# A graph layer on one core: q's node rows picked by one-hot matmuls, receivers of a group in one DMA, edge features in four pieces

## The chip, the cores and the metric

The kernel runs on one core of one Trainium2 chip. The metric is device time in microseconds (us). Before the change it is 2856.44 us, the median of three runs (2854.62 to 2858.7).

## The reference

One layer of message passing on a graph of 6,250 nodes (rows of `x`, 128 features, 8 heads of 16) and 206,250 edges, sorted by receiver. Each edge has a sender, a receiver, a weight and two sets of 32 features.

```
w_ij  = silu(edge_attr_32 @ rad_W1 + rad_b1) @ rad_W2 + rad_b2
      + silu(edge_attr_32_n2 @ sph_W1 + sph_b1) @ sph_W2 + sph_b2
q_i   = (x @ Wq)[receivers]; k_j = (x @ Wk)[senders]; v_j = (x @ Wv)[senders]
alpha = sum over a head's 16 features of q_i * w_ij * k_j, / 4, * edge_weight
out   = segment_sum(alpha * v_j, receivers) / 16
result = layernorm(x + out)          # no scale, no shift
```

All of it is float32. The inputs come sorted by receiver, so the receivers of neighbouring edges lie in a narrow band of nodes.

## The kernel before

**Units.** A tile has 128 edges, a quad four tiles (512 edges), a group four quads (2,048 edges). There are 101 groups (g = 0 to 100) and 403 quads. Within a group the quads go in the order 0, 2, 1, 3, which are slots 0 to 3 of the loop. Quads 0 and 2 (slots 0 and 1) form one pair for the hidden layers, quads 1 and 3 the other.

**Before the loop.** `x` is turned and multiplied with Wk and Wv; the rows of k and v go to a table in DRAM, `kv_tab`. `tables` (L252) works out small tables: for each quad the first node of a window of 32 nodes (`qb`), for each group the first node of a window of 128 nodes (`gb`). The receiver numbers relative to the quad's window (`rel`) are also turned and stored in DRAM (`rel_lin`).

**The loop.** An edge's q is not gathered. For each group the 4 x 32 rows of x of its quads' windows are loaded (`load_q`, L153: four DMAs of 32 rows, each with its start read into a register of SP, L117), turned by one transpose on TensorE (`turn_q`, L336, copied to SBUF by ScalarE at L338) and multiplied with Wq (`make_q`, L344, L346). `take_q` (L388) then multiplies q's 32 rows with a one-hot matrix of the receivers (`hotT`, L350, made by VectorE from `relb`, the receivers spread over 32 partitions per quad by `load_rel`, L145, in four DMAs).

For a quad, TensorE runs the hidden layers of both feature sets (`hidden`, L367: contraction over 32 rows, so the two quads of a pair use four separate strips of rows), ScalarE takes the silu (L372), TensorE multiplies by the second weights (`weigh`, L379) and ScalarE adds the bias (L381). VectorE multiplies by q (L393), TensorE turns the product back to edges in rows (`turn_back`, L399), VectorE multiplies by k (L404), sums per head (L406), multiplies by the weight (L407) and multiplies v by the result (`messages`, L415). TensorE adds the messages by receiver with one-hots (`sum_quads`, L425), a group's sums are placed in its window of 128 nodes and joined with those of the group before (`sum_group`, L446, L448, ScalarE's copy `tot` at L450), and `statistics` (L463 and on) adds the window's rows of x (`xw`, loaded by `load_xw`, L452) and normalizes. The rows go out to DRAM for four groups at a time (L479), in slot 2 of the groups with g % 4 = 1.

**What sets the order.** Each engine's order is the order of the code (a manual schedule); semaphores are derived from it. SP issues all plain DMAs in that order too, one after another: a DMA that has to wait for its buffer holds back those behind it. In slot 0 of group g SP gets `load_q(g+1)`, `load_xw(g-1)` and `load_rel(g+1)`, in slot 1 `load_feats(g+2)`. Most tiles of a group have two buffers, so `feats` of group g+2 goes where that of group g was. GpSimd issues only the gathers of k and v (L113): four DMAs per quad, 14 quads ahead of their use, into a ring of 16 buffers; the four gathers of a new quad wait until `messages` (L415) has read the buffer. The four `ph` buffers in PSUM are shared in turn by hidden layers, `weigh`, `sum_group`, `turn_q` and `make_q`.

Where TensorE's work is placed in a slot:

```
w = weigh(q)
if before is not None:
    pu = turn_back(before)
pq = take_q(q)
if slot % 2 == 0:
    ...
        hidden(pairs[u])
if slot == 1 and 2 <= g:
    sum_group(g - 2)
if slot == 1 and g + 1 < NG:
    turn_q(g + 1)
if slot == 3:
    make_q(g + 1)
```

`sum_quads(g - 1, ...)` follows in every slot from the second group on, and then VectorE's work.

Of the kernel before, what the change touches and what calls it, by code (L numbers as in the profile page):

```python
# [22 lines left out]
P = 128  # L23
N = 6250
# [27 lines left out]
def gnn_kernel(ctx, tc, x, src, dst, weight, edges, rad_W1, rad_b1, rad_W2, rad_b2,  # L52
# [35 lines left out]
    ones = const.tile([P, P], F32, name="ones")  # L88
    eps = const.tile([P, 1], F32, name="eps")
    rel = const.tile([P, NT], F32, name="rel")  # L90
    qb_i = const.tile([1, NG * NQ], I32, name="qb_i")
    gb_i = const.tile([1, NG], I32, name="gb_i")
    rowq = const.tile([P, NG], F32, name="rowq")
    rowp = const.tile([P, NG], F32, name="rowp")
    gb = const.tile([P, NG], F32, name="gb")
# [28 lines left out]
    for q in order:  # L124
        if q % NQ < 2:
            pairs.append([q])
        else:
            pairs[-1].append(q)
    feats_of, relb_of, act_of, kv_of, hot_of, hotT_of, xq_of, q_of, msg_of = ({} for _ in range(9))
    po_of, part_of, to_of, tot_of, xw_of, y0_of, u_of = ({} for _ in range(7))  # L130

    def gathers(q):
        kv = quad_of("kv", RING, 2 * D)
# [1 line left out]
            gather(kv[:, t, :], kv_tab, src_i[:, q * QT + t:q * QT + t + 1])  # L135
        kv_of[q] = kv

    def load_feats(g):
        feats_of[g] = gp.tile([P, EG // 2], F32, name="feats")
        nc.sync.dma_start(feats_of[g], edges[g])  # L140

    def quads_in(g):
        return min(NQ, QUADS - g * NQ)

    def load_rel(g):  # L145

        relb_of[g] = gp.tile([P, EQ], BF16, name="relb")
        for j in range(NQ):
            t = g * GT + j * QT
            nc.sync.dma_start(relb_of[g][j * W:(j + 1) * W, :],  # L150
                              rel_lin[t:t + QT, :].rearrange("t e -> (t e)").partition_broadcast(W))

    def load_q(g):  # L153

        xq_of[g] = gp.tile([P, D], F32, name="xq")
        for j in range(quads_in(g)):
            r = start_of(qb_i, g * NQ + j, N - W)
            nc.sync.dma_start(xq_of[g][j * W:(j + 1) * W, :], x[ds(r, W), :])

    manual = ctx.enter_context(ExitStack())  # L160
    manual.enter_context(tc.manual_schedule())
# [15 lines left out]
    with tc.tile_pool(name="nodes", bufs=1) as nodes, \  # L177
            tc.tile_pool(name="nodes_ps", bufs=2, space=PSUM) as nps:
        chunks = [(c, min(QT, NB - c)) for c in range(0, NB, QT)]
        quads_x = order[:XQ]  # L180
        xs_of, xT_of = {}, {}
        smalls = []
        for i, (w, b, bb) in enumerate(((rad_W2, rad_b1, rad_b2), (sph_W2, sph_b1, sph_b2))):
            smalls += [(w2[:, i, :], w), (b1[:, i:i + 1], b[:, None]), (b2[:, i:i + 1], bb[:, None])]
# [1 line left out]
            smalls.append((w1[i * R:(i + 1) * R, :], w))  # L186


        def load_x(k):
# [61 lines left out]

        def tables():  # L252
            nc.vector.tensor_scalar(gb, qb[:, :, 0], float(N - P), None, op0=OP.min)
            nc.vector.tensor_copy(qb_i, qb[:1].rearrange("p g j -> p (g j)"))
            nc.vector.tensor_copy(gb_i, gb[:1])
            load_q(0)
            for j in range(NQ):
                b = slice(j * W, (j + 1) * W)
                nc.vector.tensor_scalar(roww[b, :], row[b, :], float(j * W), None, op0=OP.subtract)
                nc.vector.tensor_tensor(rowq[b], qb[b, :, j], gb[b], op=OP.subtract)  # L260
            nc.vector.tensor_scalar(rowq, rowq, roww, None, op0=OP.add)
            nc.vector.tensor_copy(rowwp, roww)
            nc.vector.tensor_copy(colp, col)

# [31 lines left out]
        for _ in range(12):  # L296
            nc.tensor.transpose(warm[:, :P], ident, ident)
        for k in range(8):
            load_x(k)
# [5 lines left out]
        for i, (k, n) in enumerate(work):  # L305
            if i + 2 < len(work):
                turn(*work[i + 2])
            kvs = k_and_v(k, n)
            for o, w in smalls[i:i + 1]:
                nc.scalar.dma_start(o, w)  # L310
            if i >= len(chunks):
                kv_of[k[0]] = kvs
                continue
            store(k, kvs)
            if k + 8 < len(chunks):
                load_x(k + 8)
# [13 lines left out]


    with tc.tile_pool(name="ps", bufs=1, space=PSUM) as pp:
        def turn_q(g):
            n = quads_in(g) * W
            pt = pp.tile([P, EQ], F32, name="ph", bufs=4)
            nc.tensor.transpose(pt[:, :n], xq_of[g][:n, :], ident[:n, :n])  # L336
            xq_of[g] = gp.tile([P, P], F32, name="xqT")
            nc.scalar.activation(xq_of[g][:, :n], pt[:, :n], AF.Copy)  # L338

        def make_q(g):  # L340

            n = quads_in(g) * W
            pt = pp.tile([P, EQ], F32, name="ph", bufs=4)
            nc.tensor.matmul(pt[:n, :D], xq_of[g][:, :n], wq, start=True, stop=True)  # L344
# [14 lines left out]
        def hidden(pair):  # L359

            for q in pair:
                g, j = divmod(q, NQ)
                r0, c0 = 2 * R * (j // 2), EQ * (j % 2)
                for i in range(2):
                    ph = pp.tile([P, EQ], F32, name="ph", bufs=4)
                    r = slice(r0 + i * R, r0 + (i + 1) * R)
                    nc.tensor.matmul(ph, w1[r, :], feats_of[g][r, c0:c0 + EQ], start=True, stop=True)  # L367
                    act_of[q, i] = ph
            for q in pair:
                for i in range(2):  # L370
                    act = ep.tile([P, EQ], F32, name="act", bufs=8)
                    nc.scalar.activation(act, act_of[q, i], AF.Silu, bias=b1[:, i:i + 1])  # L372
                    act_of[q, i] = act
# [75 lines left out]
            tot_of[g] = gp.tile([P, D], F32, name="tot")  # L449
            nc.scalar.activation(tot_of[g], ph[:, :D], AF.Copy)  # L450

        def load_xw(g):  # L452
            r = start_of(gb_i, g, N - P)
            xw_of[g] = gp.tile([P, D], F32, name="xw")
            nc.sync.dma_start(xw_of[g], x[ds(r, P), :])

        def statistics(g):
            first = g // LB * LB if g < NG - 2 else g
            if g == first:
                y0_of[g] = (gp.tile([P, LB, D], F32, name="y0"), gp.tile([P, LB, 2], F32, name="mv"))  # L460
            y0, mv = y0_of[first]
            k = g - first + 1
            nc.vector.tensor_tensor(y0[:, k - 1, :], tot_of[g], xw_of[g], op=OP.add)  # L463
            st = gp.tile([P, 6], F32, name="st")
            nc.vector.bn_stats(st, y0[:, k - 1, :])
            nc.vector.bn_aggr(mv[:, k - 1, :], st)
            if k == LB or g >= NG - 3:
                sd = gp.tile([P, LB], F32, name="sd")
                nc.scalar.activation(sd[:, :k], mv[:, :k, 1], AF.Sqrt, bias=eps)
                rs = gp.tile([P, LB], F32, name="rs")  # L470
                nc.vector.reciprocal(rs[:, :k], sd[:, :k])
                shift = gp.tile([P, LB], F32, name="shift")
                nc.vector.scalar_tensor_tensor(shift[:, :k], mv[:, :k, 0], -1.0, rs[:, :k],
                                               op0=OP.mult, op1=OP.mult)
                for i in range(k):
                    nc.scalar.activation(y0[:, i, :], y0[:, i, :], AF.Identity,  # L476
                                         scale=rs[:, i:i + 1], bias=shift[:, i:i + 1])
                    r = start_of(gb_i, first + i, N - P)
                    nc.sync.dma_start(out[ds(r, P), :], y0[:, i, :])  # L479
# [16 lines left out]
        def verdict():  # L496
# [4 lines left out]
            nc.vector.tensor_reduce(found, pe[:1, :8], AX.X, OP.add)  # L501
            nc.vector.tensor_scalar(general, found, 0.0, None, op0=OP.is_gt)

        turn_q(0)
        make_q(0)
        one_hots_T(0)
# [5 lines left out]
        for g in range(NG):  # L512
            last = g == NG - 1
            for slot, j in enumerate((0, 2, 1, 3)):
# [32 lines left out]
                before = q  # L547
                if slot == 0:
                    if g + 1 < NG:
                        load_q(g + 1)  # L550
                    if 1 <= g:
                        load_xw(g - 1)
                        if g + 1 < NG:
                            load_rel(g + 1)
                if slot == 1:
                    if g + 2 < NG:
                        load_feats(g + 2)
                    if 1 <= g:
                        place(g - 1)
                    if last:  # L560
                        place(g)
                        load_xw(g)
# [179 lines left out]
```

## Time and profile before

| | |
|---|---|
| median of three runs | 2856.44 us |
| the profiled execution | 2843.93 us |
| its span, first to last instruction | 2841.9 us |
| mean granted TensorE clock | 0.847 |
| gathers of k and v, GpSimd, 1,580 | 1498.5 us busy, 948 ns each |
| `weigh`, TensorE, 1,612 instructions | 961.9 us busy, 726 ns each |
| hidden layers, TensorE, 1,612 | 626.3 us busy, 726 ns each |
| `take_q`, TensorE, 806 | 475.8 us busy, 671 ns each |
| silu, ScalarE, 806 | 500.4 us busy |
| VectorE, all | 1412.9 us busy |
| DMA | 310.42 MB, 109 GB/s on average |
| DMA issues of `feats` | 101, 512 KB each |
| DMA issues of `relb` | 404, 32 KB each |
| DMA issues of `xq` / `xw` | 403, 16 KB each / 101, 64 KB each |

How to read the profile's lines: a group of instructions has its line in the kernel, its engine, the operation, output and input tiles, the count after an x, then busy time in us, the mean of one in ns, and after the next bar the idle time of that engine just before them with what ended most of it. PE is TensorE, PEld its weight loads, DVE VectorE, ACT ScalarE, POOL GpSimd, SP SyncE; "q" behind an engine is its queue of DMA issues. A float32 matmul stands in the trace as two instructions, a transpose as one. Ends of matmuls are modelled. "issue" is idle time for which no releaser shows, "remote" one whose releaser is unknown. The row PEclk gives the granted TensorE clock in tenths for 40 slices of the span. A timeline lists start, duration, engine, line, operation and, in brackets, the idle time before it. A view of windows gives each engine's busy time in stretches between two times, the granted clock, the share in which the DMA engines are busy, and GB/s.

### The profile page before, as it was taken

Reading aid. Unit: us, or ns where it says so; the run is one execution under the profiler, and the core shown is the slowest. Engines: PE = TensorE matmul, PEld = TensorE weight load, DVE = VectorE, ACT = ScalarE, POOL = GpSimd, SP = SyncE. Lnnn points to the kernel's source line nnn. Section 1 sums busy time; section 2 is a strip of 40 time slices with the busy share of each in tenths; the row PEclk is TensorE's granted clock in tenths of the full one; section 3 lists DMA queues with packets and bytes.
Section 4 is the critical chain, followed back from the end, with each engine's and each line's share of the span. In section 5 each row is a group of like instructions: output and inputs, shape, how many; then the busy total and the mean of one; then the engine's idle time right before and its main releaser. Section 6 shows DMA issues by size and latency. Waiting matters only on the chain. (4 is left out here: it accounts for less than half of the span.)

```text
span 2841.9 us, 32012 instructions
## 1 busy us (share of the span) xinstructions
PE 2310.3 (81%) x9843; PEld 1023.9 (36%) x9843; DVE 1412.9 (50%) x2874; ACT 1000.3 (35%) x1826; POOL 1530.0 (54%) x1620
## 2 busy tenths in 40 slices
PE   5578878878887888888888888888888878788887
PEld 4333333333333333333333333333333333333333
DVE  3244554555554544545454454554544545455456
ACT  1233333333332433333333343333333333333334
POOL 4455555555555555555555555555555555555540
PEclk7788988888788887878888888888888888888889
DMA  5433333333333333333333333333334333333330
GB/s 175 133 111 97 118 105 114 113 102 111 118 105 111 102 118 102 110 111 104 110 107 112 116 98 110 119 102 120 108 99 119 103 106 116 107 112 113 108 99 26
DMA packets 166844, 310.42 MB, mean 109 GB/s; under 512 B 46530, under 2 KB 99212, under 8 KB 166668
## 3 DMA queue, kind: packets, MB, share of 16 engines
q0 software_dynamic: 76864, 209.29, 25.4%
q1 hardware_dynamic: 88316, 98.64, 10.5%
q8 instruction: 79, 1.29, 0.2%
q14 instruction: 97, 0.79, 0.1%
q10 hardware_dynamic: 1488, 0.40, 0.1%
HBM read 294.70 MB, written 13.46 MB: 108 GB/s over the span
## 5 line engine op out<-in xcount | busy, mean ns | idle before, releaser
L113 POOL DMA_INDIRECT kv<-kv_tab,src_i x1580 | 1498.5, 948 | 1217.7 <-DVE msg L415 748.5
L379 PE MATMUL ph<-act,w 128*128 128x512 f32 x1612 | 961.9, 726 | 95.8 <-ACT act L372 73.5
L404 DVE TENSOR_TENSOR m<-pu,kv 128x512 f32<-128x512 f32 x403 | 278.7, 691 | 1240.3 <-remote 434.1
L367 PE MATMUL ph<-feats,w 32*128 32x512 f32 x1612 | 626.3, 726 | 259.6 <-ACT w L381 198.4
L372 ACT ACTIVATE act<-ph,b 128x512 f32<-128x512 f32 x806 | 500.4, 688 | 317.6 <-PE ph L367 222.8
L381 ACT ACTIVATE w<-ph,bsum 128x512 f32<-128x512 f32 x403 | 276.9, 687 | 758.4 <-PE ph L379 286.7
L379 PEld LDWEIGHTS ph<-act,w 128*128 128x128 f32 x1612 | 325.1, 224 | 524.0 <-issue 367.4
L388 PE MATMUL pq<-hotT,q 32*128 32x512 f32 x806 | 475.8, 671 | 2.6 <-issue 2.6
L367 PEld LDWEIGHTS ph<-feats,w 32*128 32x128 f32 x1612 | 202.8, 206 | 454.9 <-ACT w L381 269.6
L399 PEld LDWEIGHTS pu<-ident,u 128*128 128x128 f32 x1612 | 215.1, 151 | 350.9 <-issue 200.6
L399 PE MATMUL pu<-ident,u 128*128 128x128 f32 x1612 | 259.5, 286 | 86.5 <-DVE u L393 83.7
L393 DVE TENSOR_TENSOR u<-pq,w 128x512 f32<-128x512 f32 x403 | 274.8, 682 | 55.1 <-PE ph L367 39.6
L406 DVE TENSOR_REDUCE side<-m 128x32 f32<-128x512 f32 x403 | 280.1, 695 | 13.7
L415 DVE TENSOR_TENSOR msg<-kv,side 128x512 f32<-128x512 f32 x403 | 273.0, 677 | 0.0
L425 PE MATMUL po<-msg,hot 128*32 128x128 f32 x3224 | 173.1, 312 | 2.9 <-ACT part L441 2.9
L450 ACT ACTIVATE tot<-ph 128x128 f32<-128x128 f32 x101 | 28.0, 277 | 399.3 <-remote 138.2
L388 PEld LDWEIGHTS pq<-hotT,q 32*128 32x128 f32 x806 | 123.2, 191 | 76.4 <-issue 76.4
L425 PEld LDWEIGHTS po<-msg,hot 128*32 128x32 f32 x3224 | 77.6, 117 | 154.2 <-issue 136.7
L407 DVE TENSOR_TENSOR side<-side,scale 128x32 f32<-128x32 f32 x403 | 80.4, 199 | 13.8
L346 ACT ACTIVATE q<-ph 128x128 f32<-128x128 f32 (+1 forms) x101 | 28.0, 277 | 144.8 <-issue 66.1
L350 DVE TENSOR_TENSOR hotT<-relb,side 128x512 f32<-128x512 bf16 x101 | 68.8, 681 | 0.0
L355 DVE TENSOR_TENSOR hot<-rel,side 128x512 f32<-128x512 f32 x101 | 68.8, 681 | 0.0
(83 smaller groups left out, 813.2 us busy)
## 6 DMA issues: line engine op xcount, KB each, us to landing
feats<-in_edges SPq DMA_DIRECT2D x101, 512.0 KB
kv<-kv_tab,src_i POOLq DMA_INDIRECT x1580
relb<-rel_lin SPq DMA_DIRECT2D x404, 32.0 KB
xw<-in_x SPq DMA_DIRECT2D x101, 64.0 KB
out<-y SPq DMA_DIRECT2D x101, 64.0 KB
xq<-in_x SPq DMA_DIRECT2D x403, 16.0 KB
kv_tab<-kv SPq DMA_DIRECT2D x12, 512.0 KB
act<-in_x SPq DMA_DIRECT2D x12, 256.0 KB
```

Of the source, the lines that this page charges most:

```text
L113: nc.gpsimd.indirect_dma_start(out=o, out_offset=None, in_=table, in_offset=bass.IndirectOffsetOnAxis(ap=index, axis=0))
L367: nc.tensor.matmul(ph, w1[r, :], feats_of[g][r, c0:c0 + EQ], start=True, stop=True)
L372: nc.scalar.activation(act, act_of[q, i], AF.Silu, bias=b1[:, i:i + 1])
L379: nc.tensor.matmul(pw, w2[:, i, :], act_of[q, i], start=(i == 0), stop=(i == 1))
L381: nc.scalar.activation(w, pw, AF.Identity, bias=bsum)
L388: nc.tensor.matmul(pq, q_of[g][b, :], hotT_of[g][b, :], start=True, stop=True)
L393: nc.vector.tensor_tensor(u_of[q], pq, w, op=OP.mult)
L399: nc.tensor.transpose(pu[:, t, :], u_of[q][:, t * P:(t + 1) * P], ident)
L404: nc.vector.tensor_tensor(m, pu, kv_of[q][:, :, :D], op=OP.mult)
L406: nc.vector.tensor_reduce(alpha, m.rearrange("p t (h e) -> p t h e", e=HD), AX.X, OP.add)
L415: nc.vector.tensor_tensor(msg_of[q].rearrange("p t (h e) -> p t h e", e=HD), kv_of[q][:, :, D:].rearrange("p t (h e) -> p t h e", e=HD), a ...
L425: nc.tensor.matmul(po_of[g][j * W:(j + 1) * W, :], hot_of[g][:, j * QT + t, :], msg_of[g * NQ + j][:, t, :], start=(t == 0), stop=(t == QT ...
```

## The change

Three edits, with the rest following from them.

- q's nodes. The four 32-row loads `xq` and the later load `xw` of the group's 128 rows are replaced by one load of those 128 rows, `x_of[g]`, a group ahead, kept in five buffers until `statistics` adds it. A new tile `off` holds, for each quad and each of the 128 rows, the row's place in the quad's window (row number plus the group's start minus the quad's start); VectorE compares it with the column numbers (`pick`), which gives a 128 x 128 one-hot, and `turn_q` multiplies the rows by it in place of the transpose. The result is the same turned matrix. The integer table `qb_i` goes; `tables` makes `off` with two operations.
- Receivers. `load_rel` reads a group's receivers in one DMA whose source is repeated 32 times for each of four quads.
- Features. The group's tile of 128 x 1024 becomes two of 128 x 512 (quads 0 and 2, quads 1 and 3). Each is loaded in two pieces of 64 rows, and the loop issues one piece in each slot instead of the whole in slot 1.

```
+    off = const.tile([P, NG, NQ], F32, name="off")

-    def load_feats(g):
-        feats_of[g] = gp.tile([P, EG // 2], F32, name="feats")
-        nc.sync.dma_start(feats_of[g], edges[g])
+    def load_feats(g, parts=range(4)):
+        for k in parts:
+            i, b = k // 2, slice(k % 2 * 2 * R, (k % 2 + 1) * 2 * R)
+            if k % 2 == 0:
+                feats_of[g, i] = gp.tile([P, EQ], F32, name=f"feats{i}")
+            nc.sync.dma_start(feats_of[g, i][b, :], edges[g, b, i * EQ:(i + 1) * EQ])

     def load_rel(g):
         relb_of[g] = gp.tile([P, EQ], BF16, name="relb")
-        for j in range(NQ):
-            t = g * GT + j * QT
-            nc.sync.dma_start(relb_of[g][j * W:(j + 1) * W, :],
-                              rel_lin[t:t + QT, :].rearrange("t e -> (t e)").partition_broadcast(W))
-    def load_q(g):
-        xq_of[g] = gp.tile([P, D], F32, name="xq")
-        for j in range(quads_in(g)):
-            r = start_of(qb_i, g * NQ + j, N - W)
-            nc.sync.dma_start(xq_of[g][j * W:(j + 1) * W, :], x[ds(r, W), :])
+        r = rel_lin[g * GT:(g + 1) * GT, :].rearrange("(j t) e -> j (t e)", j=NQ)
+        nc.sync.dma_start(relb_of[g], r[:, None, :].to_broadcast([NQ, W, EQ]))
+    def load_x(g):
+        r = start_of(gb_i, g, N - P)
+        x_of[g] = gp.tile([P, D], F32, name="x", bufs=5)
+        nc.sync.dma_start(x_of[g], x[ds(r, P), :])

     def tables():
...
-            nc.vector.tensor_copy(qb_i, qb[:1].rearrange("p g j -> p (g j)"))
-            load_q(0)
+            load_x(0)
...
+            nc.vector.tensor_tensor(off, gb[:, :, None].to_broadcast([P, NG, NQ]), qb, op=OP.subtract)
+            nc.vector.tensor_scalar(off, off, row, None, op0=OP.add)

+        def pick(g):
+            n = quads_in(g)
+            pick_of[g] = gp.tile([P, NQ, W], F32, name="pick")
+            nc.vector.tensor_tensor(
+                pick_of[g][:, :n, :], colp[:, None, :W].to_broadcast([P, n, W]),
+                off[:, g, :n, None].to_broadcast([P, n, W]), op=OP.is_equal)
         def turn_q(g):
-            nc.tensor.transpose(pt[:, :n], xq_of[g][:n, :], ident[:n, :n])
+            nc.tensor.matmul(pt[:, :n * W], x_of[g], pick_of[g][:, :n, :], start=True, stop=True)

                 if slot == 0:
                     if g + 1 < NG:
-                        load_q(g + 1)
-                    if 1 <= g:
-                        load_xw(g - 1)
-                        if g + 1 < NG:
+                        load_x(g + 1)
+                        pick(g + 1)
+                        if 1 <= g:
                             load_rel(g + 1)
+                if g + 2 < NG:
+                    load_feats(g + 2, (slot,))
                 if slot == 1:
-                    if g + 2 < NG:
-                        load_feats(g + 2)
                     if 1 <= g:
                         place(g - 1)
```

In the order of the engines' instructions, GpSimd's and ScalarE's are the same as before, TensorE's too but for the operands of `turn_q`; VectorE has one `pick` more per group, behind slot 0's `messages`; SP has fewer.

More of the change, by code (lines that the diff above doesn't have):

```diff
@@ L90, in gnn_kernel @@
     rel = const.tile([P, NT], F32, name="rel")
-    qb_i = const.tile([1, NG * NQ], I32, name="qb_i")
     gb_i = const.tile([1, NG], I32, name="gb_i")
+    off = const.tile([P, NG, NQ], F32, name="off")
     rowq = const.tile([P, NG], F32, name="rowq")
@@ L128, in gnn_kernel @@
             pairs[-1].append(q)
-    feats_of, relb_of, act_of, kv_of, hot_of, hotT_of, xq_of, q_of, msg_of = ({} for _ in range(9))
-    po_of, part_of, to_of, tot_of, xw_of, y0_of, u_of = ({} for _ in range(7))
+    feats_of, relb_of, act_of, kv_of, hot_of, hotT_of, x_of, q_of, msg_of = ({} for _ in range(9))
+    po_of, part_of, to_of, tot_of, xT_of, y0_of, u_of, pick_of = ({} for _ in range(8))
     def gathers(q):
@@ L180, in gnn_kernel @@
         quads_x = order[:XQ]
-        xs_of, xT_of = {}, {}
+        xs_of = {}
         smalls = []
@@ L186, in gnn_kernel, with load_nodes @@
             smalls.append((w1[i * R:(i + 1) * R, :], w))
-        def load_x(k):
+        def load_nodes(k):
             c, n = chunks[k]
@@ L298, in gnn_kernel @@
         for k in range(8):
-            load_x(k)
+            load_nodes(k)
             if k == 5:
@@ L315, in gnn_kernel @@
             if k + 8 < len(chunks):
-                load_x(k + 8)
+                load_nodes(k + 8)
             if k == 4:
@@ L332, in gnn_kernel @@
     with tc.tile_pool(name="ps", bufs=1, space=PSUM) as pp:
+        def pick(g):
[4 more added lines that the diff above has]
+                off[:, g, :n, None].to_broadcast([P, n, W]), op=OP.is_equal)
         def turn_q(g):
-            n = quads_in(g) * W
+            n = quads_in(g)
             pt = pp.tile([P, EQ], F32, name="ph", bufs=4)
-            nc.tensor.transpose(pt[:, :n], xq_of[g][:n, :], ident[:n, :n])
-            xq_of[g] = gp.tile([P, P], F32, name="xqT")
-            nc.scalar.activation(xq_of[g][:, :n], pt[:, :n], AF.Copy)
+            nc.tensor.matmul(pt[:, :n * W], x_of[g], pick_of[g][:, :n, :], start=True, stop=True)
+            xT_of[g] = gp.tile([P, P], F32, name="xT")
+            nc.scalar.activation(xT_of[g][:, :n * W], pt[:, :n * W], AF.Copy)
         def make_q(g):
@@ L343, in make_q @@
             pt = pp.tile([P, EQ], F32, name="ph", bufs=4)
-            nc.tensor.matmul(pt[:n, :D], xq_of[g][:, :n], wq, start=True, stop=True)
+            nc.tensor.matmul(pt[:n, :D], xT_of[g][:, :n], wq, start=True, stop=True)
             q_of[g] = gp.tile([P, D], F32, name="q")
@@ L362, in hidden @@
                 g, j = divmod(q, NQ)
-                r0, c0 = 2 * R * (j // 2), EQ * (j % 2)
+                r0 = 2 * R * (j // 2)
                 for i in range(2):
@@ L366, in hidden @@
                     r = slice(r0 + i * R, r0 + (i + 1) * R)
-                    nc.tensor.matmul(ph, w1[r, :], feats_of[g][r, c0:c0 + EQ], start=True, stop=True)
+                    nc.tensor.matmul(ph, w1[r, :], feats_of[g, j % 2][r, :], start=True, stop=True)
                     act_of[q, i] = ph
@@ L450, in sum_group @@
             nc.scalar.activation(tot_of[g], ph[:, :D], AF.Copy)
[L452 to L455, printed above, removed]
         def statistics(g):
@@ L462, in statistics @@
             k = g - first + 1
-            nc.vector.tensor_tensor(y0[:, k - 1, :], tot_of[g], xw_of[g], op=OP.add)
+            nc.vector.tensor_tensor(y0[:, k - 1, :], tot_of[g], x_of[g], op=OP.add)
             st = gp.tile([P, 6], F32, name="st")
@@ L502, in verdict @@
             nc.vector.tensor_scalar(general, found, 0.0, None, op0=OP.is_gt)
+        pick(0)
         turn_q(0)
@@ L561, in gnn_kernel @@
                         place(g)
-                        load_xw(g)
                 if slot == 2 and g + 1 < NG:
```

## The prediction

> **What bounds it now.** The page first. TensorE is the busiest engine and its granted clock is not full; GpSimd's gathers and VectorE's product `m` (L404) come with large idle times.
>
> ```profile
> PE 2310.3 (81%) x9843; PEld 1023.9 (36%) x9843; DVE 1412.9 (50%) x2874; ACT 1000.3 (35%) x1826; POOL 1530.0 (54%) x1620
> PEclk7788988888788887878888888888888888888889
> L113 POOL DMA_INDIRECT kv<-kv_tab,src_i x1580 | 1498.5, 948 | 1217.7 <-DVE msg L415 748.5 <-issue 425.0 <-DVE kv L220 36.6
> L404 DVE TENSOR_TENSOR m<-pu,kv 128x512 f32<-128x512 f32 x403 | 278.7, 691 | 1240.3 <-remote 434.1 <-PE ph L379 250.4 <-PE pu L399 208.5
> ```
>
> An average says little here, so I cut the trace at each group's first L379 matmul and asked for the windows of single groups (columns: us, then busy time of PE, PEld, DVE, ACT, POOL with counts, granted clock, DMA share, GB/s). Groups 31, 34 and 99:
>
> ```profile
> 961.30:988.60 27.30, 22.86 (x100) 9.61 (x96) 13.49 (x28) 8.71 (x16) 15.15 (x16) 0.87 0.35 107
> 1043.20:1065.10 21.90, 19.61 (x97) 9.24 (x96) 11.87 (x24) 9.03 (x15) 13.97 (x15) 0.92 0.47 140
> 2791.20:2809.80 18.60, 17.82 (x103) 8.43 (x95) 13.48 (x29) 8.71 (x17) 0.00 (x0) 1.00 0.03 7
> ```
>
> The same work takes 27.3 us in one group and 18.6 us in another. Of the groups from 2 to 96, 48 of 95 take 27.2 to 27.8 us, their mean is 27.19 us; groups 98 and 99, after the last gather, take 19.8 and 18.6. Some 8 us a group, nearly 800 us in all, are lost while gathers run. Where, the timeline of group 31 shows (start, us, instruction, idle before):
>
> ```profile
> 970.11 0.39 PE L448 MATMUL ph<-tot,to 128*128 128x128 f32 x2
> 975.19 0.94 POOL L113 DMA_INDIRECT kv<-kv_tab,src_i  x1 [0.30 <-issue]
> 975.50 0.28 ACT L450 ACTIVATE tot<-ph 128x128 f32<-128x128 f32 x1 [6.42 <-PE ph L367]
> 976.43 0.94 POOL L113 DMA_INDIRECT kv<-kv_tab,src_i  x1 [0.30 <-issue]
> 976.95 0.28 ACT L338 ACTIVATE xqT<-ph 128x128 f32<-128x128 f32 x1 [1.16 <-PE ph L367]
> 979.92 0.69 ACT L381 ACTIVATE w<-ph,bsum 128x512 f32<-128x512 f32 x1 [2.70 <-PE ph L367]
> 979.98 0.69 DVE L404 TENSOR_TENSOR m<-pu,kv 128x512 f32<-128x512 f32 x1 [7.79 <-PE ph L367]
> 983.09 0.94 POOL L113 DMA_INDIRECT kv<-kv_tab,src_i  x1 [5.71 <-DVE msg L415]
> ```
>
> `tot` needs only L448, which ends at 970.50, and starts 5.0 us later. In group 99 the same pair reads thus:
>
> ```profile
> 2800.16 0.39 PE L448 MATMUL ph<-tot,to 128*128 128x128 f32 x2
> 2800.58 0.28 ACT L450 ACTIVATE tot<-ph 128x128 f32<-128x128 f32 x1 [1.44 <-PE ph L448]
> ```
>
> There it starts 0.03 us after. So PE's results are announced late while gathers run, and all that PE waits for back (the `ph` buffers of the next hidden layers, freed by `tot`, `xqT`, `w`) is late too. GpSimd had issued since 962.66 without a pause, twelve gathers, one every 1.25 us; at 977.4 it runs out of free `kv` buffers, and some 2.5 us later all is released at once. Over the trace, PE's signals are late mostly from 8 us into such a run to 2.5 us after it. Then the clock pays too:
>
> ```profile
> 978.80:985.60 6.80, 5.05 (x14) 1.88 (x14) 4.05 (x9) 3.11 (x5) 1.90 (x3) 0.50 0.11 34
> ```
>
> Half clock for 6.8 us of this group. The Trainium skill, "TensorE: Matmul & The Clock Gate", Part 1, says the gate falls to half after an idle window of some 3.4 us and that gaps alone bring this; the row agrees (two such windows after the gap). By it any shorter gap would give back the 6.8 us at half speed as well, 3.4 us a group; no number below uses it.
>
> Last the waits of SP's queue, which the change empties:
>
> ```profile
> SPq L140 <- PE ph L367: 493.8, 63, 18.2
> SPq L455 <- DVE st L465: 463.9, 66, 16.5
> SPq L479 <- ACT y L476: 443.6, 25, 21.7
> ```
>
> They are long, yet almost nobody waits for what SP loads: only L336 does, 7.0 us put down to the `xq` DMA and 21.5 us to issue (16 times, 28.5 us).
>
> **The change, part by part.**
>
> *q's nodes.* The transpose L336 becomes a float32 matmul with x as weights and the one-hot as moving operand. The rows:
>
> ```profile
> L336 PE MATMUL ph<-ident,xq 128*128 128x128 f32 x100 | 29.8, 298 | 29.3 <-issue 21.5 <-DMA xq<-in_x 7.0 <-ACT act L372 0.6
> L344 PE MATMUL ph<-wq,xqT 128*128 128x128 f32 x200 | 49.4, 330 | 3.0 <-issue 3.0
> ```
>
> L344 is what it becomes: two instructions a matmul, 0.49 us in the timeline against 0.27. So 0.22 x 101 = 22 us more on PE. It stands in slot 1 right after L448. In groups like 31 PE then waits 8 us for signals, which hides it; in the other half it shows: 11 us (bounds 0 and 22). On VectorE comes `pick`, 128x128 compare, not in the trace; nearest are L463 (128x128 tensor_tensor, 288 ns) and L435 (128x128 compare from the same PSUM tile, 345 ns). 101 times 0.29 to 0.35 is 29 to 35 us, but it stands behind slot 0's messages, where VectorE then waits about 2 us for PE (L404's 1240 us of idle time); I take 0, and 29 to 35 if that cover goes. Queued behind it is slot 1's `m`. turn_q's new wait for `pick` is met over 3 us ahead, as the slot between is some 5 us. Of the 28.5 us at L336, up to all goes, since x is loaded a group earlier and waits for no buffer that is still read (five of them); what is late next there is PE's own signal, so I take half: -14 (bounds -28.5 and 0).
>
> *SP's queue.* Four register loads, four 16 KB DMAs and a second 64 KB load become one register load and one DMA; four `relb` DMAs become one; one `feats` DMA becomes four. Eleven DMAs a group (with `out`'s one) become seven. In group 31 the four `xq` issues took 5.76 us of SP, without gathers (at 2777.62) 2.81. The new queue is shorter, and the wait of L455 disappears. But nobody waits for this queue beyond the 28.5 us already taken: 0. Before the loop, `tables` gains two 128x404 operations for a cast of 351 ns; L239's 579 ns prices them, so +0.8 us, and its DMAs save about 2 us of SP's 3.04: -1 together.
>
> *The pieces of feats.* Each buffer half is freed by one pair of hidden layers, so pieces 0 and 1 are freed together in slot 2, pieces 2 and 3 in slot 0; SP runs ahead and issues them in pairs of 256 KB, not one per slot. After stores of `out` (every fourth group) piece 3, x and receivers stand behind ScalarE's y, up to 21.7 us (L479), but are needed later than that. Same bytes: 0.
>
> *Receivers in one DMA.* Its source's slowest dimension counts 4, not 32. The page "DMA: Bandwidth & Descriptors", Rules for kernel authors, says such a DMA is confined to at most four of the sixteen engines. By its 27 GiB/s an engine 32 KB would take an estimated 1.1 us each instead of 0.3. No run here shows one yet. From the trace alone: DVE idles 0.0 us before L350, its only reader, a group later, so 0, and a few us late would still be hidden.
>
> **Sum.** 2843.93 (span 2841.9 and 2 around it) + 11 - 14 - 1 = 2840, bounds by the same terms 2814 (0 - 28.5 - 1) to 2900 (22 + 35 - 1). The median of the runs is 12.5 us above this execution, so I state 2850 for the median, 2827 to 2912.
>
> **Rivals.**
>
> *A, the sum: 2850.* For it: the gathers, their order and the buffers that release them are untouched, and groups with g % 4 = 1, in which SP waits at L479 and issues next to nothing, lose as much (mean 27.32). Against it: the groups are a coupled cycle, and small shifts decide between 20 and 32 us.
>
> *B, the runs of gathers break up: 2750.* Groups with g % 4 = 2 average 26.09 us, some 20.0 to 21.9: feats comes late there, the signals of PE are late already at 7.5 us into the run, so GpSimd runs dry after eight gathers and the stall is short. With 256 KB instead of 512 KB after slot 0, more groups may go so. All groups at 26.1: 95 x 1.1 = 105 us less, 2750. If GpSimd never starved PE, its 16 x 1.25 = 20 us a group would be the floor, near 2200.
>
> *C, slower: 2930.* Fewer disturbances leave all groups in the 27.4 us cycle (+17 us), with the 22 us of PE shown: 2895. And where 0.22 us more PE work, or the heavy bursts after stores, push a release past the next change of the clock, a group gets one more half-clock stretch (3.4 us): in a quarter of the groups +81 us, 2937. It decides from more than one group in ten on. For it: the clock's stretches and the 27.3 us go together; against: PE's extra work stands ahead of the stall.
>
> *D, the pieces or receivers arrive late*: one 64-row piece late per group would show as a wait of L367 on a DMA, of which there is none now. Taken into C.
>
> **Chances.** A 0.45, B 0.28, C and D 0.27. A measurement can tell about 0.2% (6 us) from no change. A is centred 6 us below the median: faster 0.21, same 0.12, slower 0.12 of it. With B and C: faster 0.49, same 0.12, slower 0.39. For 8 in 10 the range goes to B's 2750 and some beyond it, and to C's 2930: 2720 to 2930; A's own is 2827 to 2912.
>
> **What would show it.** The profile after: granted clock near 0.85, groups still mostly at 27.3 us, `tot` 2 to 5 us behind its matmul during runs of twelve gathers; turn_q's matmul at 0.49 us without a DMA wait ahead of it; `pick` at 0.3 us with no idle time moved onto L404; SP's L455 wait gone. Runs of eight gathers in most groups and a clock above 0.9 would mean B; half-clock stretches of 10 us in many groups, C. I am wrong outright if transfers from SP, and not the gathers, delay PE's signals: then halving SP's work would bring far more than 100 us.

## The result, and the profile after

The changed kernel takes 2865.18 us (median of 20 runs, 2848.79 to 2884.36) beside 2855.2 us of the kernel before (20 runs, 2848.66 to 2861.37; the record names no chip for this comparison): ratio 1.0031, 95% interval 1.002 to 1.0042. It is slower, by 0.31% or about 9 us. The forecast was 2850, faster; the time lies within the range of 2720 to 2930, which is wide because it was made for B and C; the sign is wrong.

The page of the changed kernel, the same lines as were shown of before (a page names one releaser for a group); L415 is now the product `m`:

```profile
span 2882.6 us, 30627 instructions
...
PE 2366.4 (82%) x9944; PEld 1049.1 (36%) x9944; DVE 1431.8 (50%) x2976; ACT 1004.1 (35%) x1826; POOL 1525.2 (53%) x1620
...
PEclk7788888989889888888897888988988889889879
...
L113 POOL DMA_INDIRECT kv<-kv_tab,src_i x1580 | 1493.9, 945 | 1252.4 <-DVE msg L426 755.4
...
L415 DVE TENSOR_TENSOR m<-pu,kv 128x512 f32<-128x512 f32 x403 | 278.5, 691 | 1268.5 <-remote 569.3
```

The profiled execution took 2884.36 us, the slowest of its 20. Its span is 40.7 us above the one shown of before, four times what the medians differ by, so a difference between these two profiles is read for its kind and not for its size. TensorE's 56 us more are the hidden layers, 682.1 us (before 626.3); in e1 below, the fastest, they are 669.0, so this does not follow the time. `turn_q` went from 30.0 to 40.8 us. The granted clock is 0.853, before 0.847.

By themselves `pick` costs what was priced and `turn_q`'s matmul half of it. The matmul's row among the lines, then the same from the view of the tile `x` (count, then duration in ns min/median/max, first and last start, shapes), and the tile `pick`:

```profile
L347 PE MATMUL ph<-pick,x 128*128 128x128 f32 x200 | 40.4, 285 | 7.3 <-issue 7.3
```

```profile
L347 PE MATMUL ph<-pick,x x202: 248/275/582, 113.4 to 2840.6; 128*128 128x128 f32 x100, 128*128 128x96 f32 x1
L340 DVE TENSOR_TENSOR pick<-side,off x101: 248/282/285, 94.3 to 2836.6; 128x128 f32<-128x128 f32 x100, 128x96 f32<-128x96 f32 x1
```

Two instructions of 0.275 us, which overlap in part, against one of 0.27, and 0.28 us for `pick`. No DMA ends TensorE's idle time ahead of L347, and SP's queue no longer waits for a load of x; what is left there are the pieces and the stores of `out` (waits of SP's queue: total us, times, longest):

```profile
SPq L145 <- PE ph L378: 1351.3, 126, 14.1
SPq L485 <- ACT y L482: 490.9, 25, 41.5
```

What bounds the kernel is unchanged. Windows of the changed kernel (us, then PE, PEld, DVE, ACT, POOL busy, clock, DMA share, GB/s): group 41, group 34, and the half-clock stretch that begins in group 34:

```profile
1251.50:1278.70 27.20, 21.51 (x100) 9.57 (x96) 14.00 (x31) 11.81 (x23) 15.11 (x16) 0.87 0.29 86
1056.80:1087.00 30.20, 26.48 (x101) 10.83 (x97) 14.79 (x30) 10.05 (x18) 15.13 (x16) 0.79 0.43 123
1074.40:1091.50 17.10, 16.80 (x41) 6.53 (x40) 7.51 (x15) 5.31 (x10) 6.96 (x8) 0.50 0.23 64
```

Most groups take 27.2 us with 6.8 us at half clock, as before; six stretches of half clock last 17.1 us, in before's profile three. Mean over groups 2 to 96: 27.48 us, before 27.19. By the place in the pattern of four (g % 4 = 0, 1, 2, 3) the means are 27.02, 27.23, 27.59 and 28.07 us, before 27.93, 27.32, 26.09 and 27.41: the groups right behind the stores (g % 4 = 2), the short ones in before, are no longer short.

### The profile page after: what moved, and what is told of

It reads as the page before. It is cut to its first block, busy times and chain, and to the rows that moved or that the text cites. A ratio compares the mean times of both kernels' runs of the same rounds, so it can differ in the third digit from the quotient of the medians.

```text
span 2882.6 us, 30627 instructions
## 1 busy us (share of the span) xinstructions
PE 2366.4 (82%) x9944; PEld 1049.1 (36%) x9944; DVE 1431.8 (50%) x2976; ACT 1004.1 (35%) x1826; POOL 1525.2 (53%) x1620
## 3 DMA queue, kind: packets, MB, share of 16 engines
q8 instruction: 80, 1.31, 0.2%
## 4 chain that ended last, share of the span: by engine, by line
PE 75%; another core or an unknown queue 13%; ACT 6%; issue 4%; DVE 2%; DMA 0%; SPq 0%; DVEq 0%; ACTq 0%
PE ph L390 30%; PE ph L378 17%; PE pq L399 12%; PE pu L410 6%; PE po L436 5%; ACT act L383 2%; ACT w L392 2%; PE ph L355 1%; PE ph L457 1%; PE pk L221 1%; PE ph L347 1%; PE ph L459 1%; ACT tot L461 0%; DVE u L404 0%
## 5 line engine op out<-in xcount | busy, mean ns | idle before, releaser
L390 PE MATMUL ph<-act,w 128*128 128x512 f32 x1612 | 946.3, 716 | 87.2 <-ACT act L383 76.3
L378 PE MATMUL ph<-feats,w 32*128 32x512 f32 x1612 | 682.1, 713 | 335.2 <-ACT w L392 228.1
L415 DVE TENSOR_TENSOR m<-pu,kv 128x512 f32<-128x512 f32 x403 | 278.5, 691 | 1268.5 <-remote 569.3
L399 PE MATMUL pq<-hotT,q 32*128 32x512 f32 x806 | 464.9, 657 | 0.0
L378 PEld LDWEIGHTS ph<-feats,w 32*128 32x128 f32 x1612 | 213.9, 203 | 573.5 <-ACT w L392 316.3
L417 DVE TENSOR_REDUCE side<-m 128x32 f32<-128x512 f32 x403 | 280.1, 695 | 13.7
L349 ACT ACTIVATE xT<-ph 128x128 f32<-128x128 f32 (+1 forms) x101 | 27.9, 277 | 149.7 <-PE ph L378 77.2
```

The costliest lines, as they stand in the source:

```text
L378: nc.tensor.matmul(ph, w1[r, :], feats_of[g, j % 2][r, :], start=True, stop=True)
L390: nc.tensor.matmul(pw, w2[:, i, :], act_of[q, i], start=(i == 0), stop=(i == 1))
L399: nc.tensor.matmul(pq, q_of[g][b, :], hotT_of[g][b, :], start=True, stop=True)
L415: nc.vector.tensor_tensor(m, pu, kv_of[q][:, :, :D], op=OP.mult)
L417: nc.vector.tensor_reduce(alpha, m.rearrange("p t (h e) -> p t h e", e=HD), AX.X, OP.add)
```

## The experiments

The runs below fell on five chips, called A to E here; each ratio is against the kernel before on the same chip. The chip of the first comparison is not on record. It was most likely not A: the granted clock of before's profile there was 0.847, and 35 executions of before on A had 0.857 to 0.866. That profile is also the only one of before; on A to E before was timed and not profiled. The chips matter: on A, B and C the kernel before takes 2849 to 2856 us, on D and E 2076 and 2080. "T" in the expectations is this theory: the gathers delay TensorE's signals, that stall sets a cycle of 27.3 us, and the change costs by disturbing SP's queue less, so that more groups keep the full cycle (at first with the pieces as the part that does most of it). Its rivals: "R1", TensorE's added work costs; "R2", the single receivers DMA costs. "S" stands for two things: in e5 and e6 for the rival that SP's transfers or the order of the work delay the signals, in e14 to e16 for the theory that the stores of `out` hold SP's queue.

Three counts from the traces are used below. *Locked*: the share of groups 2 to 96 of 27.1 to 27.8 us. *Half clock*: us at a granted clock of 0.5 from group 2 on. *Late*: the share of TensorE's semaphore events more than 0.12 us after the modelled end of their instruction, among those that the trace holds (1,971 of 2,523 in before).

### The parts, one by one (chip A)

`e1_q_alone` is the kernel before with the q edit only (`load_x`, `off`, `pick`, `turn_q`); `e2_receivers_alone` and `e3_feats_alone` have one edit each; `e4_q_and_receivers` is the changed kernel without the pieces:

```
e2:
-        for j in range(NQ):
...
+        r = rel_lin[g * GT:(g + 1) * GT, :].rearrange("(j t) e -> j (t e)", j=NQ)
+        nc.sync.dma_start(relb_of[g], r[:, None, :].to_broadcast([NQ, W, EQ]))
e3:
+                if g + 2 < NG:
+                    load_feats(g + 2, (slot,))
                 if slot == 1:
-                    if g + 2 < NG:
-                        load_feats(g + 2)
```

> Only q's nodes are picked by one-hots (one load of 128 rows a group, no xq, no xw); receivers stay in four DMAs and feats in one. Theory T (the change loses because it takes away what broke up the long runs of gathers: after the stores of out, feats came late and the following group had runs of eight gathers instead of twelve): feats still stands behind the stores here, so runs of eight stay, and this part alone gives 0 to -28 us (the waits of L336 go). Rival R1 (TensorE's 22 us of extra matmul is the loss): +9 us or more, the whole loss. Rival R2 (the relb DMA on four engines or the small feats pieces are slow): 0.

> Only the receivers of a group come in one DMA. T: 0 within 4 us, as nobody waits for relb; at most the runs of gathers shift. R1: 0. R2 in its first form (a DMA confined to a few engines is late or in the way of the gathers): +5 us or more, and idle time of VectorE ahead of hotT.

> Only feats comes in four pieces. T: three pieces no longer wait behind the stores in the group after them, so twelve-gather runs grow (77 in the profile after, 53 before) and runs of eight shrink; most of the loss is here, +8 to +25 us. R1: 0. R2 in its second form: a wait of L367 on a feats DMA shows, +5 us or more.

> The change without the four pieces of feats. T: the sum of the first two runs, 0 to -28 us, so the pieces are what makes the whole change slower. R1: +9 us or more, the whole loss, as in the q part alone. R2: between the two.

Measured beside before's 2855.5:

| kernel | us | ratio, interval | mean group | locked | half clock |
|---|---|---|---|---|---|
| q | 2851.17 | 0.9989, 0.9978 to 0.9999 | 27.24 | 0.87 | 668 |
| receivers | 2857.25 | 1.0007, 0.9995 to 1.0019 | 27.31 | 0.78 | 698 |
| pieces | 2858.56 | 1.0008, 0.9993 to 1.0023 | 27.34 | 0.79 | 709 |
| q and receivers | 2858.77 | 1.0016, 1.0006 to 1.0027 | 27.34 | 0.81 | 712 |

(The first comparison's profiles, likely of another chip: before 27.19, 0.49, 787; the changed kernel 27.48, 0.65, 762.) The q edit by itself gains 3 us; receivers and pieces cannot be told from nothing alone, and the pieces do not bring most of the loss here. The parts do not add: by the means of the runs, q with receivers lies 6.2 us (95% interval 3.5 to 9.0) above before plus the two single differences. T has its sign wrong where it can be seen best: the kernel with the most locked groups is the fastest. Locking by itself is not what costs.

### What sets the 27 us (chip B)

`e5_no_gathers` leaves out the gathers of k and v inside the loop and uses the rows of the first 14 quads again:

```
-                    gathers(order[i + AHEAD])
+                    kv_of[order[i + AHEAD]] = kv_of[order[(i + AHEAD) % AHEAD]]
```

> Before, with the gathers in the loop left out (the rows of k and v of the first 14 quads are used again and again); all other loads and all arithmetic stay. Theory T (gathers on GpSimd delay TensorE's signals and so set the group's time): groups of 18.6 to 20 us as after the last gather, clock 1.0, 125 + 101 x 19.2 = about 2070 us. Rival S (SP's transfers, or the order of the work, delay them): 27 us a group stay, 2840 us.

2050.44 us, one run, before 2850.8. Its page:

```profile
span 2048.7 us, 29289 instructions
...
PE 1878.2 (92%) x9843; PEld 902.7 (44%) x9843; DVE 1408.0 (69%) x2874; ACT 1003.0 (49%) x1826; POOL 54.8 (3%) x64
...
PEclk7889999999999999999999999999999999999998
```

Groups take 18.6 to 19.9 us, 22 us are at half clock, and 5% of TensorE's signals are late instead of 44%. On this chip the gathers cost 800 us.

`e7_half_the_bytes` gathers 512 bytes a row instead of 1,024 (rows of x stand for k and for v):

```
-            gather(kv[:, t, :], kv_tab, src_i[:, q * QT + t:q * QT + t + 1])
+            gather(kv[:, t, :D], x, src_i[:, q * QT + t:q * QT + t + 1])
```

> Before, with each gather bringing 512 bytes a row instead of 1024 (rows of x in place of k, and the same half read for v): same number of gathers and of their issues, half the bytes. T with the issue as cause: groups of 27 us stay, 2840 us. T with the bytes as cause (the DMA engines or their completion): clearly fewer late signals, 22 us a group, about 2350 us.

2855.76, one run: the same. The bytes are not it, which leaves the number of gathers, or their issue.

`e8_turn_three_times` does before's transpose three times, 27 us more of TensorE in all (57.0 us busy, before 30.0) where the change adds 11:

```
-            nc.tensor.transpose(pt[:, :n], xq_of[g][:n, :], ident[:n, :n])
+            for _ in range(3):
+                nc.tensor.transpose(pt[:, :n], xq_of[g][:n, :], ident[:n, :n])
```

> Before, with turn_q's transpose made three times, which adds about 0.22 us of TensorE work a group at the place of the change, as the one-hot matmul does. Prediction's step: hidden in the stall, 0 to +11 us. Rival R1: +22 us.

2851.46 beside 2850.8, ratio 1.0001 (0.9969 to 1.0033). No cost shows, within 9 us either way, where R1 asked for 22; with e1's gain this speaks against R1.

### Pacing the gathers (chips B and C)

A memset on GpSimd behind each gather (`e6_gathers_spaced` 128x128, `e11_pause_per_gather` 128x256), or one of 128x768 behind each quad's four (`e12_pause_per_quad`):

```
+    idle = const.tile([P, 256], F32, name="idle")
...
             gather(kv[:, t, :], kv_tab, src_i[:, q * QT + t:q * QT + t + 1])
+            nc.gpsimd.memset(idle, 0.0)
```

> Before, with a memset of 128x128 on GpSimd behind each gather (some 0.25 us, the pitch goes from 1.25 to about 1.5 us, 24 us a group). T in its strong form (what delays the signals is that issue goes on without a pause): signals are late less often, groups fall towards 24 to 26 us, 2550 to 2750 us. T in its weak form (each gather delays them, whatever the pitch): GpSimd runs dry later, the stall is as long as the run of twelve, now 18 us instead of 15, and groups take 30 us and more, 3100 us. S: 0.

> The kernel before with a memset of 128x256 on GpSimd behind every gather, twice that of e6: pitch of the gathers near 1.5 us instead of 1.25 (1.34 in e6), 24 us of GpSimd per group. If signals of TensorE are late because gathers are issued faster than they are worked off (a backlog that grows in a run), a pitch of 1.5 shortens or ends the stall: groups at 24 to 25 us, 2550 to 2650 us. If any unbroken run of gathers delays the signals whatever the pitch, the runs only get longer: 2850 to 2950 us.

> The kernel before with one memset of 128x768 on GpSimd behind each quad's four gathers: a pause of about 1.2 us every 5 us, GpSimd busy some 24 us per group. If a short pause lets the delayed signals through (in the trace they are late only from 6 to 8 us of unbroken issue on), no run reaches the point where signals are late: groups of 20 to 24.5 us, 2300 to 2650 us. If 1.2 us is too short to clear them (after a run's end signals clear in 1 to 2.5 us), the stall stays: 2840 to 2950 us.

e6 lies mostly in the 0.30 us gap that follows each gather anyway: pitch 1.34 us instead of 1.25, 2849.81, ratio 0.9991 (0.996 to 1.0022). With e11 the pitch is 1.45 us and the time 2656.84, ratio **0.9325** (0.9294 to 0.9355); with e12 2790.59, 0.9794 (0.9765 to 0.9823), two executions each. e11 ends just above the range expected of a backlog, e12 between its two ranges. GpSimd's groups in e11:

```profile
L114 POOL DMA_INDIRECT kv<-kv_tab,src_i x1580 | 1509.9, 956 | 506.4 <-issue 247.3 <-DVE msg L417 222.8 <-DVE kv L222 36.0
L137 POOL MEMSET idle<- 128x256 f32 x1580 | 519.0, 328 | 0.9
```

GpSimd has 519 us more to do and the kernel is 190 us faster: its wait for `messages` falls from 748.5 to 222.8 us. Late signals by their place in an unbroken run of gathers: in before some 45% at 6 to 8 us, 82% at 8 to 10, over 90% beyond; in e11 some 12%, a third, and 60% only at 12 to 16 us. The share over the whole trace is hardly less (42%). In e12 no run is longer than four gathers and yet 75% are late at 4 to 5 us: a pause of 0.76 us does not clear what has piled up. What piles up is not told by the trace: packets of the gathers go on starting at the pace of the issues.

### Two parts at a time (chip C)

`e9_q_and_pieces` is the changed kernel with before's four receivers DMAs, `e10_receivers_and_pieces` is e3 with the single one.

> The change without the single receivers DMA (four DMAs of relb as before). Measured so far against before: q alone 0.9989, receivers alone 1.0007, pieces alone 1.0008, q with receivers 1.0016, all three 1.0031. If the parts simply add, 0.9989 x 1.0008 = 0.9997, 2855 us. If the loss comes from an interaction of any two edits that empty SP's queue (theory T: fewer disturbances, more groups in the 27.3 us cycle), about 1.002, 2861 us. If the receivers' single DMA is what costs (rival R2), at or under 1.000.

> The change without the q picks (xq loads, transpose and xw as before; receivers in one DMA, feats in four pieces). If the parts add, 1.0007 x 1.0008 = 1.0015, 2860 us. By theory T (an emptier queue locks more groups in the cycle) 1.0015 to 1.003. If the q edit is needed for the loss (its matmul, pick or missing DMAs), at most 1.0005.

e9 2886.64, ratio 1.0118 (1.0094 to 1.0142); e10 2879.51, 1.0108 (1.0081 to 1.0135); before 2849.36. Locked 0.39 and 0.33, half clock 818 and 822 us, mean group 27.61 and 27.46. Larger than any expectation, larger than all three parts together, and with few locked groups: T does not fit here either. e10 has no q edit and e9 has the four receivers DMAs, so here neither of these is needed for a loss of 1%; what both have is the pieces. The pieces alone were not run on this chip, so either two edits interact, or the pieces cost more on C than on A (1.0008).

### Another kind of chip (chips D and E)

`e14_stores_act_before`, `e15_stores_act_q_pieces` and `e16_stores_act_after` issue the stores of `out` from ScalarE's queue in before, in e9 and in the changed kernel; `e13_after_paced` is the changed kernel with e11's memset:

```
-                    r = start_of(gb_i, first + i, N - P)
-                    nc.sync.dma_start(out[ds(r, P), :], y0[:, i, :])
+                    r = start_of(gb_i, first + i, N - P, ACT)
+                    nc.scalar.dma_start(out[ds(r, P), :], y0[:, i, :])
```

> The changed kernel with e11's memset of 128x256 on GpSimd behind every gather. Pacing alone brought before to 0.9325 [0.9294, 0.9355] of before (2656.84 us). If the change has a cost of its own, 0.935 or more, 2665 us up; if its +0.31% comes only from the stall's cycle, the same as e11 within about 1%, 0.925 to 0.940; if its few saved waits pay once the stall is shorter, under 0.925.

> The kernel before with the stores of out, and the register load of their row, on ScalarE's queue instead of SP's. Theory S (the stores hold SP's queue and so set the pattern of four groups): the pattern goes, all groups near 27.3 us, 2850 to 2865 us, 0.998 to 1.004. Rival (the stores do not matter): pattern and time as before, 1.000. The issue itself costs ScalarE about 1 us per store, 100 us in all, beside its long idle times.

> e9 (q and pieces, 1.0118) with the stores on ScalarE's queue. Theory S: the loss goes, within 0.3% of e14. Rival (something else in the two edits together costs 1%): 1.009 to 1.014 as e9.

> The changed kernel (1.0031) with the stores on ScalarE's queue. Theory S: within 0.2% of e14. Rival: 0.3% or more above e14.

Chip D ran the kernel before in 2075.95 us (11 runs, 2067.76 to 2081.65), so none of these four tests its question about a stalling chip. e13 2360.06, ratio 1.1379 (1.134 to 1.1418): pacing, worth 6.75% on chip C, makes GpSimd the bound here (VectorE's `m` waits 673 us for gathers, 295 times). e14, e15, e16: 2228.36, 2232.42, 2235.97, ratios 1.0742, 1.076, 1.0772, intervals of plus or minus 0.3 to 0.4% each. About 150 us for moving the four stores that stand in every fourth group: in e14 groups take 18.63 us, but the one behind the stores 28.56 on average. By themselves the three do compare on one chip: with the stores off SP's queue the changed kernel (e16) is 7.6 us above before's (e14), near the 11 us that its ordinary groups add (18.74 beside 18.63), and no gain shows. Windows of its groups 33 and 34, then ScalarE in group 34:

```profile
756.20:774.80 18.60, 17.82 (x99) 8.46 (x95) 12.66 (x27) 9.81 (x18) 14.03 (x16) 1.00 0.49 148
774.80:804.90 30.10, 22.88 (x100) 10.18 (x96) 14.81 (x31) 12.07 (x22) 18.36 (x20) 0.77 0.40 120
```

```profile
774.84 0.34 ACTq L480 DMA_DIRECT2D out<-y  x1
...
781.37 0.35 ACTq L480 DMA_DIRECT2D out<-y  x1
781.76 0.69 ACT L382 ACTIVATE w<-ph,bsum 128x512 f32<-128x512 f32 x1 [1.98 <-DMA out<-y]
```

From the second store on, ScalarE's next instruction waits for the store ahead of it (1.31, 1.76 and 1.98 us), `w` (L382) starts 6.9 us after the first issue, and group 34 gets a half-clock stretch of 13.7 us.

Then `e17_after_again`, the changed kernel itself, and `e18_q_and_pieces_again`, the kernel of e9, went together to one chip.

> The changed kernel, on the same chip as e18. Where the signals stall (before at 2850 us): if the parts interact, 1.002 to 1.004 as in the first comparison while e18 stays near 1.012; if the earlier sizes were those of the chips, both have the same ratio within 0.3%. Where they do not stall (before at 2076 us): the change's own cost shows, 0.995 to 1.004, since the waits it removes (28.5 us at most) and the work it adds (22 us of TensorE, 28.5 us of VectorE) are of one size.

> q with pieces, the receivers in four DMAs (e9 again), on the same chip as e17. Where the signals stall: 1.009 to 1.014 if e9's loss belongs to the kernel; the ratio of e17 within 0.3% if it belongs to the chip. Where they do not stall: the ratio of e17 within 0.2%, since the single receivers DMA is then the only difference and nobody waits for it.

It was chip E, with before at 2079.88 (11 runs, 2077.89 to 2092.78). The changed kernel takes 2044.62, ratio **0.9827** (0.9803 to 0.9851): faster by 1.7%, outside the expected 0.995 to 1.004. e18 takes 2046.17, 0.9837 (0.981 to 0.9863): the single receivers DMA makes no difference that shows. The page of e17:

```profile
span 2044.4 us, 30627 instructions
...
PE 1903.1 (93%) x9944; PEld 924.1 (45%) x9944; DVE 1432.0 (70%) x2976; ACT 1005.0 (49%) x1826; POOL 1527.0 (75%) x1620
...
PEclk9999999999999999999999999999999999999998
```

The same program with the same gathers (946 ns each here, 945 there) has 4% late signals here and 40% in the first profile. It is read most quickly from who ended ScalarE's idle time ahead of `tot` (releaser: us, times). In the changed kernel's first profile:

```profile
  PE ph L378: 201.5, 31
  remote: 85.2, 13
...
  PE ph L459: 17.8, 9
```

and in e17:

```profile
  PE ph L459: 141.2, 96
```

`tot` needs the matmul L459. Here it is released by it 96 times; there mostly by something later, so the announcement was late.

What bounds e17 is another thing. GpSimd issues its 1,580 gathers without one pause, from 49.8 us to the end of the last at 2026.0, 1.25 us each, and the kernel ends 18 us later. TensorE's ordinary groups of 18.7 us are shorter than the 20 us in which 16 gathers are issued, so the lead of 14 quads is used up, and late in the run VectorE's product waits for rows of k and v (50 of the 54 waits come after 1600 us). From the view of the tile `kv` and that of the waits:

```profile
L113 POOL DMA_INDIRECT kv<-kv_tab,src_i x1580: 942/946/1471, 49.8 to 2025.0; - x198
```

```profile
DVE m L415 <- DMA kv<-kv_tab,src_i: 82.9, 54, 4.1
```

So on chip E the changed kernel stands at the pace of its gathers, and what more an edit of SP's queue might bring could not show.

## Why the prediction was wrong

**The bound.** That gathers delay TensorE's signals and so cost some 8 us a group held on chip B: without them 2050 us. That this belongs to the kernel did not hold: on D and E, with the same gathers, 4% of the signals are late and the kernel runs at 2045 to 2080. The prediction took a property of the chip it saw for one of the program. Rival B's floor of 16 x 1.25 = 20 us a group is what e17 reaches; the "near 2200" worked out from it was 155 us too high. One reading of the clock does not hold: that the half clock of group 31 follows an idle window. Its length fits two windows, but the 3.4 us ahead of it hold 2.30 us of TensorE's work:

```profile
975.40:978.80 3.40, 2.30 (x4) 0.58 (x4) 0.00 (x0) 0.56 (x2) 1.68 (x2) 0.99 0.39 116
```

**turn_q's matmul, "11 us (bounds 0 and 22)".** The size was 0.11 us a group and not 0.22: 40.8 us busy against 30.0. On D it shows in full, as an ordinary group of the changed kernel takes 18.74 us (e16) and one of before's loop 18.63 (e14): 11 us. On chip B e8, which adds 27 us, finds none of it within 9 us.

**pick, 0.** 0.28 us as priced, and hidden.

**L336's waits, "-14 (bounds -28.5 and 0)".** Together with the matmul the prediction had -3 for this part; the q edit alone measured -3.1 us (interval -6.3 to -0.3). By size it was right, on a chip that is likely not the one it was made for. Whether as -14 + 11 or as a smaller gain over a hidden matmul, e1 does not tell; e8 speaks for the second, and then the agreement is luck.

**The step that failed: "nobody waits for this queue beyond the 28.5 us already taken: 0", and with it the zeros for receivers and pieces, added to the q part.** Alone they are zeros on chip A: 1.0007 and 1.0008, neither told from 1. Together with another part they are not. On A the receivers' DMA, worth 2 us alone, takes 8 us beside the q edit (0.9989 to 1.0016), and the 6.2 us by which the parts fail to add are clear of the noise. On C receivers with pieces, without the q edit, take 1.0108, 30 us, where the prediction had 0 + 0. The prediction had looked at who waits for what SP loads, rightly found almost nobody, and took the edits for independent; it named the coupled cycle ("small shifts decide between 20 and 32 us") only as an argument against A and gave it no term. How the 9 us of the first comparison divide among the parts no run tells, since the parts were not run on its chip.

**What couples them** stays open. C's first mechanism, more groups in the 27.4 us cycle, does not fit: on A e1 has the most and is the fastest. For its second, a further half-clock stretch in some groups, there is one mark: on A none of e1, e2 and e3 has a half-clock stretch of 17.1 us, and e4 (q with receivers) has four, three of them behind stores. Group 46 in e4, its stretch, and group 46 in e1:

```profile
1364.60:1394.80 30.20, 25.32 (x101) 10.55 (x97) 14.71 (x30) 9.99 (x17) 15.17 (x16) 0.79 0.37 109
1382.30:1399.40 17.10, 15.08 (x42) 6.07 (x42) 7.52 (x15) 5.04 (x9) 7.07 (x8) 0.50 0.17 52
```

```profile
1367.00:1394.30 27.30, 23.51 (x100) 9.76 (x96) 13.76 (x29) 9.97 (x18) 15.14 (x16) 0.87 0.39 118
```

Four groups some 3 us longer would be 12 us, of the size of the 8 us between e4 and e1. Against it: before's first profile has three such stretches and more half clock in all than the changed kernel's (787 and 762 us), and e8 has 798 us and no loss. With one profile a kernel it is not shown to be the cause. C's price, 2930, was far too high. B did not occur: the clock stayed at 0.853. D did not either: no wait of TensorE or VectorE on a piece or on the receivers shows in the changed kernel's profile. The Trainium skill, "DMA: Bandwidth & Descriptors", Rules for kernel authors, which would have the receivers' DMA on at most four engines, is neither shown nor refuted: e17 and e18 differ in it and have 0.9827 and 0.9837.

The Trainium skill, "TensorE: Matmul & The Clock Gate", Part 1, has the gate change in windows of some 3.4 us; the stretches of 6.8 and 17.1 us are two and five such windows, and the groups of 27.3 us eight.

**Where the 35 us on chip E come from.** There is no profile of before on E, so this is worked out, not shown. With +0.11 us in 76 ordinary groups, the 25 groups behind stores must each be some 1.7 us shorter (43 / 25), if the part ahead of the loop is equal (on D it is, 63.5 us in e14 and 63.8 in e16). In e17's group 34 (SP's queue, then TensorE):

```profile
719.90 7.83 SPq L485 DMA_DIRECT2D out<-y  x4
727.79 0.48 SPq L145 DMA_DIRECT2D feats<-in_edges  x1
728.83 0.35 SPq L160 DMA_DIRECT2D x<-in_x  x1
```

```profile
731.27 0.46 PE L347 MATMUL ph<-pick,x 128*128 128x128 f32 x2 [1.43 <-DMA x<-in_x]
```

The stores hold SP for 7.8 us, and L347 waits 1.43 us for the load behind them, which is issued 1.4 us after the last store (729.18). In before the four loads with their register reads stand there, 2.8 us of SP by the prediction's figure for them without gathers: an estimate of 1.4 us later. In 25 groups that is 35 us at most, of the 43 needed, and in e17 only 11 groups show this wait (12.9 us in all). So the q edit may well pay where the prediction looked for it, at L336, where TensorE has nothing else to wait for; that this is all of the gain is not shown. e14 and e16 agree with it: with the stores on another queue the gain is gone.

**Left open.** What couples the edits on a stalling chip; whether e9's 1.0118 beside the changed kernel's 1.0031 belongs to the parts or to the chip, since both were run together only on E; whether the pieces alone cost 1% on C; whether the stores' place in SP's queue matters on a stalling chip; and what differs between the chips.

## What to carry to other kernels

When single groups of equal work take 18.6 and 27.3 us, first find what makes the slow ones, and price an edit under that cover and without it: one change was +0.31% on one chip and -1.73% on another. A saved wait is worth nothing if its engine next waits for something later than the saving. Parts that change one queue are also priced together: on chip A a DMA worth 2 us alone took 8 us beside another edit. Measure a change of a fraction of a per cent on more than one chip before it is kept or dropped; the same holds for a cure, as pacing the gathers gave 0.9325 on one chip and, in the changed kernel, 1.1379 on another.

## What the runs showed of the hardware

- The same kernel took 2849 to 2856 us on three chips and 2076 to 2080 on two, with gathers of the same length (0.945 us). What the traces show to differ is how late TensorE's semaphore events come while gathers are issued in one run: 44% late by over 0.12 us in before's profile, 4% in every profile of chips D and E. VectorE's and ScalarE's events are late in 0.2% of cases in before's profile too.
- On the chips that stall, spacing gathers from 1.25 to 1.45 us moved the point from which signals are late from 6 to 8 us of a run to 12 to 16, and saved 190 us (chip C). Spacing to 1.34 changed nothing that shows (chip B); a pause of 0.76 us after every fourth gather saved 59 us.
- With four 64 KB stores on ScalarE's queue its next instruction of the loop started 6.9 us after the first issue, and the kernel took 150 us more in all, with 280 us at half clock (e14, chip D; before has no profile there).
- TensorE's clock fell to half behind a window of 3.4 us in which it worked 2.30 us (before, group 31).
